# Cross attention: the subtraction of the row minima on GpSimd, one exponential a unit, and all transpose copies on ScalarE

## The chip, the cores and the metric

The kernel runs on one core of a Trainium2 chip. The metric is the device time of one launch in microseconds; the time before is the median of three runs. Five engines work side by side, each through its own instructions in order: TensorE (PE in the profile, its weight loads as PEld), VectorE (DVE), ScalarE (ACT), GpSimd (POOL) and SyncE (SP, which here issues DMAs). TensorE writes to PSUM[...]; GpSimd does not read PSUM in this kernel.

## The reference

One decoder layer, all in float32, for 4 batches of 1024 tokens with 256 features: a self attention made of three parts, a cross attention to 154 context rows with a distance bias, and a mixture of 8 experts with 2 for each token and a shared one. Each is followed by a residual sum and a layer norm. The change touches the cross attention alone:

```python
q = (query @ Wq.T + bq) * d ** (-0.5)      # 16 heads of 16 features
k = key_ @ Wk.T + bk                       # 154 rows
v = value @ Wv.T + bv
scores = jnp.einsum('bhqd,bhkd->bhqk', q, k)
distance_bias = -jnp.log(distances + 1e-09) * jnp.abs(distance_scaling)
scores = scores + distance_bias[:, None, :, :]
attn = jax.nn.softmax(scores, axis=-1)
out = jnp.einsum('bhqk,bhkd->bhqd', attn, v)
```

## The kernel before

The batches follow one another. Each has its self attention (long loops of score matmuls, exponentials and products), then a closing norm, then the cross attention, then a second norm. The experts come at the end, from about 2770 us on.

The cross attention of a batch is a loop over 32 units and 4 more steps (L951). A unit n is one pair of heads and one pair of token tiles: group n // 8 of four heads, token pair (n % 8) // 2, head pair n % 2. A step n emits, in this order: the scores of unit n; now and then the query projection of the next group (`project_q`, after units 3, 11 and 19); `flip` of unit n-2; on odd steps `product` of units n-5 and n-4; one piece of the next batch's beginning (`ahead`: score maxima and value projections, not in the last batch); and what the step counter `clock` has due, the `divide` of an earlier product.

`scores` (L654) makes four matmuls of 128 rows by 154 columns into one of two big PSUM buffers, which `maxima` and the projections of `ahead` use too. `biased` (L267, called at L673) is one VectorE instruction for each of the four 154-column parts (DVE L269): it reads the scores from PSUM, adds the bias, writes the negated sum to the tile `xs` and its minimum to a column of `xmx`. Four exponentials on ScalarE (L682) then work in place on `xs`, each with its own minimum as bias and scale -1, so that each gives exp(score - maximum).

`flip` (L691) transposes the unit on TensorE (L697), four 128x77 blocks into each of two small PSUM buffers (c = 0 and 1), and copies each to the tile `xpt`, 77 rows by 512 columns: on ScalarE (L705), except for c = 1 of odd units, which VectorE copies (L703). There are three small buffers, shared with `divide`, `values` and others. `product` (L708) multiplies two units by the values (L716), ScalarE copies the result to `avx` (L724), and `divide` (L348) transposes it back (L351) and divides it by the sums on VectorE (L354, L355).

The order on each engine is not only the source's. The framework orders instructions by the place in the source and by its own estimate of when each is ready and its buffer free, and writes the waits itself. Tiles of one kind share a ring of buffers: `xs`, `xpt` and the tiles of self attention share ten, `xmx` has three.

GpSimd adds the output bias to the residual just ahead of the loop (L747, eight instructions) and clears the values' tile of the next batch after it (L924). ScalarE takes the logarithm of the next batch's distances (L942) near the loop's end; the exponential and the logarithm need different function tables, each loaded by an ACT_TABLE_LOAD.

## Time and profile before

| | us |
|---|---|
| median of 3 runs (3431.95 to 3436.01) | 3435.27 |
| the profiled execution | 3433.82 |
| its span | 3432.0 |
| TensorE busy | 3300.5 |
| VectorE busy | 1725.3 |
| ScalarE busy | 1601.0 |
| GpSimd busy | 373.3 |
| first to last cross-attention score matmul, batch 0 | 632.3 to 737.4 |
| the same, batches 1, 2 and 3 | 1320.2 to 1423.6, 2006.3 to 2109.9, 2669.4 to 2754.1 |

A group's line in the profile reads: source line, engine, operation, tiles written and read, shapes, count, then after the bar the busy time and the mean in ns of one, then the idle time of that engine just ahead of it and what ended most of it. A line of the timeline reads: start, duration, engine, source line, operation, tiles, shapes, count, and in brackets the idle time and its releaser. The matmuls' ends are modelled, so that a busy TensorE need not be one at its peak. The granted clock of TensorE is 1.00 at full speed and 0.50 at half.

### The profile page before, as it was taken

How to read it: one execution, taken by the hardware profiler on the slowest of the kernel's cores; microseconds unless marked ns; L12 is line 12 of the kernel's file. 1: busy time of each engine (PE TensorE's matmuls, PEld its weight loads, DVE VectorE, ACT ScalarE, POOL GpSimd, SP SyncE). 2: the span in 40 equal slices, each digit the busy share in tenths (PEclk: the TensorE clock that was granted, in tenths of full speed). 3: DMA queues.
4: the chain of work that ended last, by engine and by line, in shares of the span. 5: the costliest groups of instructions: out<-in, count | busy, mean ns of one | idle time of the engine just before them, and what ended most of it. 6: DMA issues, size and time to landing. Idle time of an engine off the chain costs nothing.

```text
span 3432.0 us, 60936 instructions
## 1 busy us (share of the span) xinstructions
PE 3300.5 (96%) x25260; PEld 2085.6 (61%) x25260; DVE 1725.3 (50%) x3571; ACT 1601.0 (47%) x3130; POOL 373.3 (11%) x601
## 2 busy tenths in 40 slices
PE   7999999999999999999999999999999999999997
PEld 4555667565556675665566756555667665555554
DVE  3565555565655555656555556565556551122224
ACT  1555534375555453755554537555534731222223
POOL 4000000000000000000000000000000018222123
PEclk7999999999999999999999999999999999999999
DMA  9000000000000000000000000000000052111114
GB/s 204 1 2 1 1 1 1 3 21 14 1 1 1 1 1 3 21 13 2 1 1 1 1 3 9 1 2 1 1 1 1 1 203 82 47 42 44 44 44 157
DMA packets 75866, 84.13 MB, mean 25 GB/s; under 512 B 15136, under 2 KB 65928, under 8 KB 75592
## 3 DMA queue, kind: packets, MB, share of 16 engines
q1 hardware_dynamic: 68040, 61.53, 6.4%
q0 software_dynamic: 7552, 18.70, 1.6%
q8 instruction: 202, 3.31, 0.4%
q14 instruction: 72, 0.59, 0.1%
HBM read 46.52 MB, written 33.69 MB: 23 GB/s over the span
## 4 chain that ended last, share of the span: by engine, by line
PE 85%; DVE 9%; ACT 2%; issue 2%; POOL 1%; DMA 1%; SPq 0%; ACTq 0%; DVEq 0%; POOLq 0%
PE big L288 10%; PE big L422 8%; PE big L530 8%; PE one L566 7%; PE acc L584 7%; PE big L1226 7%; PE one L480 7%; DVE mxp L429 6%; PE one L460 4%; PE acc L1248 4%; PE one L697 3%; PE big L1178 3%; PE big L662 3%; PE one L302 2%; PE acc L716 2%
## 5 line engine op out<-in xcount | busy, mean ns | idle before, releaser
L429 DVE TENSOR_REDUCE mxp<-big 128x2 f32<-128x1024 f32 x512 | 610.3, 1218 | 305.5 <-PE acc L460 252.1
L422 PE MATMUL big<-k,q 31*128 31x512 f32 x2048 | 595.8, 644 | 30.2 <-DVE mxp L429 26.6
L471 ACT ACTIVATE ex<-one 128x512 f32<-128x512 f32 x696 | 391.3, 601 | 247.4 <-PE acc L460 182.9
L460 PE MATMUL one<-q,k 32*128 32x256 f32 x2784 | 501.9, 397 | 0.0
L269 DVE CUSTOM_DVE_ANT_0 prob<-big,zero_t 128x1024 f32<-128x1024 f32 x256 | 303.6, 1222 | 271.9 <-PE big L530 271.7
L460 PEld LDWEIGHTS one<-q,k 32*128 32x128 f32 x2784 | 326.8, 186 | 31.0 <-ACT ex L471 2.5
L549 ACT ACTIVATE prob<-prob,nmx 128x1024 f32<-128x1024 f32 x256 | 293.0, 1153 | 20.2 <-DVE nmx L269 19.7
L530 PE MATMUL big<-mk,mq 64*128 64x512 f32 x1024 | 284.4, 633 | 2.5 <-ACT ex L468 2.5
L422 PEld LDWEIGHTS big<-k,q 31*128 31x128 f32 x2048 | 180.1, 189 | 171.5 <-DVE mxp L429 93.6
L571 ACT COPY pt<-one 128x512 f32<-128x512 f32 x256 | 137.8, 588 | 311.7 <-PE one L566 311.7
L566 PEld LDWEIGHTS one<-ident,prob 128*128 128x128 f32 x2048 | 221.8, 142 | 98.1 <-issue 92.4
L1226 PE MATMUL big<-wall,xt 128*128 x576 | 272.5, 596 | 1.8 <-POOL by L1202 1.8
L460 PE MATMUL acc<-q,k 32*128 32x256 f32 x928 | 263.9, 404 | 0.0
L566 PE MATMUL one<-ident,prob 128*128 128x128 f32 x2048 | 257.6, 279 | 0.0
L480 PE MATMUL one<-ex,v 128*32 128x256 f32 x4096 | 248.4, 382 | 0.0
L1236 DVE TENSOR_TENSOR hidr<-big,slr 128x512 f32<-128x512 f32 x72 | 49.8, 691 | 332.7 <-ACT slr L1234 332.7
L682 ACT ACTIVATE xs<-xs,xmx 128x154 f32<-128x154 f32 x512 | 174.4, 414 | 69.6 <-DVE xmx L269 69.6
L480 PEld LDWEIGHTS one<-ex,v 128*32 128x32 f32 x4096 | 119.8, 110 | 122.1 <-ACT ex L471 35.8
L573 DVE COPY pt<-one 128x512 f32<-128x512 f32 x256 | 164.3, 683 | 10.9 <-PE one L566 10.9
L269 DVE CUSTOM_DVE_ANT_0 xs<-big,bias 128x154 f32<-128x154 f32 x512 | 132.0, 314 | 66.0 <-ACT avx L724 33.5
L530 PEld LDWEIGHTS big<-mk,mq 64*128 64x128 f32 x1024 | 99.6, 191 | 101.7 <-issue 79.4
L460 PEld LDWEIGHTS acc<-q,k 32*128 32x128 f32 x928 | 155.4, 186 | 0.0
(266 smaller groups left out, 4715.2 us busy)
## 6 DMA issues: line engine op xcount, KB each, us to landing
xg<-scratch SPq DMA_DIRECT2D x72, 129.0 KB, 2.0
scratch<-empty SPq DMA_DIRECT2D x1, 9216.0 KB
r<-result SPq DMA_DIRECT2D x8, 1024.0 KB, 11.2
y<-in_x_dram SPq DMA_DIRECT2D x4, 1024.0 KB, 5.3
wall<-in_L_ffn_w_gate_dram SPq DMA_DIRECT2D x8, 512.0 KB, 10.3
wall<-in_L_ffn_w_up_dram SPq DMA_DIRECT2D x8, 512.0 KB, 10.8
wall<-in_L_ffn_w_down_dram SPq DMA_DIRECT2D x8, 512.0 KB, 11.6
bias<-in_fside_BxSxS_dram SPq DMA_DIRECT2D x4, 616.0 KB, 4.5
```

Source lines behind the costliest of these rows:

```text
L269: nc.vector.tensor_tensor_reduce(out=out, in0=ps, in1=bias, scale=-1.0, scalar=3.0e38, op0=ALU.add, op1=ALU.min, accum_out=low,)
L288: nc.tensor.matmul(ps[:, tb, :], w[:, c, lo : lo + P], xT[:, c, tb * 512 : (tb + 1) * 512], start=(c == 0), stop=(c == NC2 - 1),)
L422: nc.tensor.matmul(ps[:, jj, :], st["q"][r : r + MR, tok : tok + P], st["k"][r : r + MR, kb * 512 : (kb + 1) * 512], start=True, stop=True,)
L429: nc.vector.reduce_max(mxp[:, t, kb, 2 * pair : 2 * pair + 2], ps, axis=AX.X)
L460: nc.tensor.matmul(scs[jj][:, i * QW : (i + 1) * QW], st["k"][r : r + MR + 1, kc * P : (kc + 1) * P], st["q"][r : r + MR + 1, part * QW : ...
L471: nc.scalar.activation(ex[:, jj, :], scs[jj], AF.Exp, scale=1.0 / HD**0.5)
L480: nc.tensor.matmul(av[32 * j : 32 * j + 32, 0:QW], self.v[:, kc, h * VW : h * VW + 32], exs[kc // 2, j // 2][:, j % 2, i : i + QW], start= ...
L530: nc.tensor.matmul(pss[i][:, kb, :], q[r : r + MD, t * P : (t + 1) * P], k[r : r + MD, kb * 512 : (kb + 1) * 512], start=True, stop=True,)
L549: nc.scalar.activation(p, p, AF.Exp, bias=nmx[:, i : i + 1], scale=-1.0, accum_out=sm[:, t % 4, i : i + 1],)
L566: nc.tensor.transpose(ps[:, kc * P : (kc + 1) * P], probs[u][i][:, at : at + P], ident)
L584: nc.tensor.matmul(av[64 * i : 64 * i + 64, (t % 4) * P : (t % 4 + 1) * P], v[:, kc, h * MD : (h + 1) * MD], flipped[u][i][:, kc, :], star ...
L1226: nc.tensor.matmul(ps[:, g, :], xt[:, c * P : (c + 1) * P], wall[:, bass.ds(off + (g * NC2 + c) * D, D)], start=(c == 0), stop=(c == NC2 - 1),
```

## The change

In `scores`, the minima tile `xmx` takes the order of `xs` (head, then token tile). One GpSimd instruction replaces `xs`, all four parts or 616 columns at once, by minimum minus negated score; the minima are read as a broadcast. One ScalarE exponential over the 616 columns, with neither bias nor scale, replaces the four. In `flip`, ScalarE makes both copies of every unit.

```diff
                 ex = ex_tile([P, 2, 2, S2], "xs")
-                mx = work.tile([P, 4], F32, tag="xmx", name="xmx", bufs=3)
+                mx = work.tile([P, 2, 2], F32, tag="xmx", name="xmx", bufs=3)
                 for tt in range(2):
                     for jj in range(2):
                         biased(
                             ex[:, jj, tt, :],
                             ps[:, jj, tt * S2 : (tt + 1) * S2],
                             self.bias[:, 2 * tp + tt, :],
-                            mx[:, 2 * tt + jj : 2 * tt + jj + 1],
+                            mx[:, jj, tt : tt + 1],
                         )
-                for tt in range(2):
-                    for jj in range(2):
-                        i = 2 * tt + jj
-                        nc.scalar.activation(
-                            ex[:, jj, tt, :],
-                            ex[:, jj, tt, :],
-                            AF.Exp,
-                            bias=mx[:, i : i + 1],
-                            scale=-1.0,
-                        )
+                nc.gpsimd.tensor_tensor(
+                    ex, mx.unsqueeze(3).to_broadcast([P, 2, 2, S2]), ex, ALU.subtract
+                )
+                nc.scalar.activation(ex, ex, AF.Exp)
                 self.ex[n] = ex
...
-                    if c == 1 and n % 2 == 1:
-                        nc.vector.tensor_copy(pt[0:HK, c, :], ps[0:HK])
-                    else:
-                        nc.scalar.copy(pt[0:HK, c, :], ps[0:HK])
+                    nc.scalar.copy(pt[0:HK, c, :], ps[0:HK])
```

## The prediction

> **What bounds the kernel now.** I read the page's busy shares first.

> ```profile
> PE 3300.5 (96%) x25260; PEld 2085.6 (61%) x25260; DVE 1725.3 (50%) x3571; ACT 1601.0 (47%) x3130; POOL 373.3 (11%) x601
> ```

> TensorE (PE) is busy nearly all the time. But shares average over stages, and the edit sits in one: the cross-attention loop, which runs four times from the first score matmul (L662) to the last product (L716), at 632.3, 1320.2, 2006.3 and 2669.4 us. The stage table cuts the first of these loops (columns: length, then busy time of PE, PEld, DVE, ACT, POOL, then the granted clock).

> ```profile
> 632.60:636.00 3.40, 2.04 (x22) 1.02 (x18) 3.17 (x17) 2.43 (x5) 0.00 (x0) 1.00 0.00 0
> 636.00:649.70 13.70, 13.70 (x39) 7.13 (x40) 5.21 (x24) 5.15 (x15) 0.00 (x0) 0.50 0.01 1
> 649.70:700.00 50.30, 49.95 (x387) 32.36 (x385) 30.84 (x135) 27.87 (x75) 0.00 (x0) 1.00 0.00 1
> 700.00:742.00 42.00, 41.96 (x409) 29.61 (x408) 26.41 (x149) 35.17 (x98) 0.00 (x0) 1.00 0.05 12
> ```

> See three phases. A head of 3.4 us in which PE idles 1.36 us. A body with no PE idle to speak of: until about 700 the next batch's matmuls are interleaved ("filled" units), after that the units stand alone ("bare") and ACT is busy 84%. And PE at half clock for 13.7 us right after the head. Is PE really the limit in the bare part, where ACT is at 84%? The chain of waits answers (start, us, what):

> ```profile
> 711.87 1.03 PE one L697 x8
> 713.12 0.72 PE big L662 x8
> 713.85 1.09 PE one L697 x8
> 714.94 1.00 PE acc L716 x16
> 715.94 0.72 PE big L662 x8
> ```

> Two units take 716.66 - 711.87 = 4.79 us, all PE: transposes, scores, transposes, product, scores, with 0.22 us for the divide's transposes at 712.90. ACT and DVE never enter. So ACT's 84% is cover, not limit.

> [...] The trace has 0.50 after a head with only 40% idle[...]; the lengths (13.7, 10.2, 10.2 and 6.8 us in the four loops) are multiples of 3.4. [...]

> **The change part by part.** There are 4 x 32 = 128 units.

> ```profile
> L682 ACT ACTIVATE xs<-xs,xmx 128x154 f32<-128x154 f32 x512 | 174.4, 414 | 69.6 <-DVE xmx L269 69.6
> L705 ACT COPY xpt<-one 77x512 f32<-77x512 f32 x192 | 104.3, 571 | 52.4 <-PE one L697 52.4
> L942 ACT ACTIVATE bias<-bias,tiny_t 128x1232 f32<-128x1232 f32 x4 | 5.3, 1322 | 7.6 <-DMA bias<-in_fside_BxSxS_dram 7.6
> ```

> ACT: four exponentials of 154 columns run in 1.36 us a unit. One of 616: between 154 columns (0.414) and 1232 (1.322) the slope is 0.842 ns a column, so 0.414 + 462 x 0.842 = 0.80 us. Saved 128 x 0.56 = 72 us. Moved to ACT are 64 copies at 0.571: 37 us added. ACT falls by 35 us net. DVE loses the 64 copies at 0.684: 44 us.

> ```profile
> L493 POOL TENSOR_TENSOR avq<-avq 128x256 f32<-128x256 f32 x64 | 46.3, 723 | 956.5 <-ACT avq L488 956.5
> L1293 POOL TENSOR_TENSOR r<-r,r 128x2048 f32<-128x2048 f32 x4 | 21.7, 5424 | 14.1 <-DMA r<-result 14.1
> ```

> POOL gains 128 subtractions of 616 columns: slope (5424 - 723)/1792 = 2.62 ns, so 0.723 + 360 x 0.00262 = 1.67 us each, 213 us in all. Broadcasting should cost nothing: POOL's copy of a broadcast 128x512 (L599) takes 613 ns, a plain one (L1124) 615. Bounds: 0.74, if the minima cost no second read (L599's 613 ns plus 104 columns at 1.2), to 2.64, if POOL stood still during DVE's 0.97 us a unit. At 2.39 us a bare unit POOL is 70% full; at 2.64 it would be the bound itself, +0.25 us on some 80 bare units, +20 us, which the range below takes in.

> All of the 35 and 44 us lies beside PE in the body, so it buys nothing. What is left is latency. Count from the end of unit n's scores. Before: 0.16 to DVE, exponentials trailing DVE by one; the last ends at about +1.9. After: DVE's four minima end at 0.16 + 1.04 = 1.20; handoff 0.16; POOL 1.67; handoff 0.12; exponential 0.80; handoff to PE 0.16: transposes may start at +4.11. They are wanted after unit n+2's scores, at +4.79. So 0.68 us is left in the bare part, and about 3 in the filled part (two units take 7.1 there, from 667.07 to 674.18). An excess x would delay only every third unit's cycle, since two more scores stand before these transposes on PE.

> Who queues behind the new wait? On ACT, the copies of unit n-2, which free PE's transpose buffers (three). If an exponential that waits for POOL stood ahead of them, they would end about +4.5 instead of 1.6 and PE would stop. In the trace the framework's order follows readiness and not the source: at 664.57 one exponential, then a copy, then three exponentials; and at 669.68 a divide's transposes lie between halves of one unit's scores. The copies are ready at +0.6, the exponential not before +2.9, so I expect the copies ahead. On POOL nothing else falls in the loop but the end of eight bias additions (626.27 to 631.79), done before the first minimum at 634.2; the next batch's memset (L924) comes after it. The c=1 copies of odd units end on ACT at about +3.6 or 4.4, before PE wants the buffer. Body: 0.

> Head: the first four exponentials ended at 636.2. Now DVE 634.2, POOL to 636.0, exponential to 636.9, or 638.1 if the 1.28 us table load is also behind the wait. PE has the next batch's maxima and values to run instead, except in the last loop. Bounds -1.4 (the idle time goes) to +3; I take +0.3 a loop. Tail: unit 31's scores ended at 737.78, so its transposes start at 737.78 + 4.11 = 741.9 and not 741.17, +0.7; its two copies are now both on ACT, +0.5 at most, and ahead of the table load and logarithm at 742.53 that hold up the last average copy. I take +0.8, between 0 and 1.5. Sum: 4 x (0.3 + 0.8) = +4.4. The profiled execution took 3433.82 (span 3432.0, 1.8 around it), 1.45 below the median of 3435.27. So 3433.8 + 4.4 = 3438.2, say **3438**, with its own range of 3429 to 3442.

> **The rivals.**
> Rival 1, **faster by the clock**: the four half-clock stretches sum to 13.7 + 10.2 + 10.2 + 6.8 = 40.9 us, costing up to 20.5. They follow heads where PE waited on single exponentials (0.29 us twice) and minima (0.78). If the new order puts other matmuls there, the head's 1.4 goes and the stretches shrink. All of it: -26; half: -13, 3421. For it: next batch's matmuls are ready in three loops. Against: the 0.78 us wait is for DVE's minima in a score buffer and stays.
> Rival 2, **slower, late ends and a cold clock**: head +3, tail +1.5, and one more half-clock window at each (1.7 us each): 4 x (4.5 + 3.4) = 32 at most, half of it +16: 3450. It decides once PE idles over about 1.4 us in 3.4, as the head does now.
> Rival 3, **slower, the new wait on ACT**: exponential n ahead of the copies of n-2. Then copies end at +4.5, the next unit's transposes and product follow (1.7 + 1.0), scores 0.72: two units take about 7.3 instead of 4.79, +2.5. Bare pairs: some 8 in each of three loops and 14 in the last, 38 in all: +95, 3529; fewer pairs give less. A subtraction beyond 1.67 + 0.68 = 2.35 us would begin a smaller stall, a third of the excess a unit.
> That the change does not do what it says has little room: the instructions are written out.

> **How the numbers follow.** Within 0.2% (6.9 us), about what a measurement of this kernel can tell from no change. My forecast 0.41, rival 1 0.27, rival 2 0.22, rival 3 0.10. The range runs from 3416 (two thirds of rival 1) to 3465 (rival 2 whole); it leaves out the end of rival 1 (0.06) and most of rival 3 (0.09). Faster 0.27, same 0.40, slower 0.33: one hundredth of the forecast's own range spills over.

> **What would show it.** Right: two bare units still 4.79 us on PE; POOL near 1.67 and ACT near 0.80 us each; copies of n-2 ahead of exponential n. Wrong: PE idle at L697 on ACT in the body (rival 3), a half-clock stretch gone or longer at the heads (rivals 1 and 2), or POOL above 2.35.

## The result and the profile after

| | before | after |
|---|---|---|
| median of 8 runs each, us | 3433.38 (3431.26 to 3436.79) | 3448.60 (3442.02 to 3452.80) |
| the profiled execution, us | 3433.82 | 3444.80 |
| its span, us | 3432.0 | 3443.0 |
| mean granted clock of TensorE in it | 0.976 | 0.973 |

After over before is 1.0042, 95% interval 1.0031 to 1.0053: slower, by about 15 us at the medians. The profiled execution after lies 3.8 us below its median, so the traces have 11.0 us to explain.

Two words for what follows: the head of a batch's loop is its first few microseconds, the tail what lies behind its last scores. The change shortens the file, so the same lines have smaller numbers after: L697 becomes L691, L716 L707, L724 L715 and L942 L933.

First the page of the kernel after, its line of busy shares.

```profile
PE 3311.8 (96%) x25260; PEld 2090.0 (61%) x25260; DVE 1684.3 (49%) x3507; ACT 1560.0 (45%) x2810; POOL 529.6 (15%) x729
```

See that three engines moved as meant: ACT lost 41 us and DVE 41, POOL gained 156. PE is busy 11.3 us longer with the same 25260 matmuls. The same matmuls took longer, and that is what a lower clock looks like, not a wait: in the kernel before, the eight 31x512 matmuls of L422 from 636.0 to 649.7 us, at a granted clock of 0.50, took 1137 ns on average, the sixteen from 649.7 to 700, at 1.00, 640 ns.

Next, the groups of instructions of the kernel after: the subtraction that is new.

```profile
L679 POOL TENSOR_TENSOR xs<-xmx,xs 128x616 f32<-128x616 f32 x128 | 155.3, 1214 | 243.3 <-DVE xmx L269 180.7
```

1.21 us each. Does PE wait for it, or for the exponential behind it? The chain of waits of the kernel after, in the bare part of batch 0 (start, us, what):

```profile
711.41 0.72 PE big L662 x8
712.14 1.03 PE one L691 x8
713.17 0.33 PE one L351 x2
713.50 0.72 PE big L662 x8
714.22 1.03 PE one L691 x8
715.25 1.00 PE acc L707 x16
716.25 0.72 PE big L662 x8
```

It is all PE, as before. Two units take 716.25 - 711.41 = 4.84 us. In PE's list of waits the transposes of the exponentials (L691) do not appear; of the loop's own lines the one that grew is the divide's transpose (L351), which waits for the copy of the average: from 4.3 us in 5 waits to 6.4 us in 6. The longest, 1.1 us before and 1.6 after, is at the tail. The timeline of the kernel after, at the end of batch 0's cross attention (start, us, engine, line, operation):

```profile
738.50 1.07 ACT L696 COPY xpt<-one 77x512 f32<-77x512 f32 x2 [0.36 <-PE one L691]
...
738.83 1.07 PE L707 MATMUL acc<-xpt,vx 77*32 77x256 f32 x16
739.59 1.28 ACT L933 ACT_TABLE_LOAD   x1
...
739.83 1.13 PE L422 MATMUL big<-k,q 31*128 31x512 f32 x4
740.88 1.32 ACT L933 ACTIVATE bias<-bias,tiny_t 128x1232 f32<-128x1232 f32 x1
742.11 0.35 ACT L715 COPY avx<-acc 128x256 f32<-128x256 f32 x1
...
742.52 0.65 PE L351 MATMUL one<-ident,avx 128*128 128x128 f32 x2 [1.55 <-ACT avx L715]
```

Read it from the bottom. PE idles 1.55 us for a copy (L715) of 0.35. The product that the copy reads ended at 739.9; ACT is then in the table load and logarithm of the next batch's bias, which came first. They in turn wait for the two copies of unit 31's transposes, now both on ACT. The same place before:

```profile
742.25 1.07 PE L716 MATMUL acc<-xpt,vx 77*32 77x256 f32 x16
...
742.53 1.28 ACT L942 ACT_TABLE_LOAD   x1
...
745.05 0.35 ACT L724 COPY avx<-acc 128x256 f32<-128x256 f32 x1
...
745.46 0.44 PE L351 MATMUL one<-ident,avx 128*128 128x128 f32 x2 [1.08 <-ACT avx L724]
```

There the table load began 0.28 us after the product (742.25 to 742.53), now it begins 0.76 us after it (738.83 to 739.59): 0.48 us later, and the idle time grew from 1.08 to 1.55.

Then the clock. The stage table of the kernel after around that gap (length, busy time of PE, PEld, DVE, ACT, POOL, then the granted clock, DMA share, GB/s):

```profile
739.20:742.60 3.40, 1.84 (x21) 0.52 (x11) 0.36 (x1) 3.23 (x4) 0.00 (x0) 1.00 0.00 0
742.60:763.10 20.50, 20.50 (x69) 12.71 (x70) 5.33 (x12) 6.21 (x10) 0.58 (x1) 0.50 0.00 0
```

Behind the window in which PE was busy 1.84 of 3.40 us, half clock follows, for 20.5 us. And the same place before:

```profile
741.20:744.60 3.40, 3.18 (x28) 1.55 (x28) 1.16 (x3) 3.04 (x4) 0.00 (x0) 1.00 0.47 142
744.60:748.00 3.40, 2.54 (x21) 1.04 (x22) 2.40 (x4) 1.17 (x3) 0.57 (x1) 1.00 0.00 0
```

No half clock followed here. I added up every half-clock stretch of both traces:

| half clock, us | before | after | change |
|---|---|---|---|
| heads of the four loops | 13.7, 10.2, 10.2, 6.8 | 10.2, 0, 13.7, 3.4 | -13.6 |
| after the first three tails | 0, 0, 3.4 | 20.5, 10.2, 13.7 | +41.0 |
| everywhere else | 120.0 | 116.5 | -3.5 |
| all | 164.3 | 188.2 | +23.9 |

I count half of a half-clock stretch as lost, an estimate from the granted 0.50 for a PE that is busy throughout: +12.0 us. (By L422's 640 and 1137 ns it would be 0.44 of a stretch, +10.5 us.) The loops bear it out. With half of 13.7, 10.2 and 10.2 us taken off, the first three loops before come to 98.6, 98.7 and 98.9 us from first to last score matmul; with half of 10.2, 0 and 13.7 taken off, those after come to 96.6, 96.8 and 96.4. With the clock taken out in this way the whole kernel before has 3349.9 us and after 3348.9. So the 11.0 us are 12.0 of clock less 1.0 of everything else.

### The profile page after: what moved, and what is told of

Read it like the earlier page. It is cut to its first block, busy times and chain, and to the rows that moved or that the text cites. A ratio compares the mean times of both kernels' runs of the same rounds, so it can differ in the third digit from the quotient of the medians.

```text
span 3443.0 us, 60727 instructions
## 1 busy us (share of the span) xinstructions
PE 3311.8 (96%) x25260; PEld 2090.0 (61%) x25260; DVE 1684.3 (49%) x3507; ACT 1560.0 (45%) x2810; POOL 529.6 (15%) x729
## 4 chain that ended last, share of the span: by engine, by line
PE 83%; DVE 9%; POOL 3%; issue 2%; DMA 2%; ACT 1%; SPq 0%; ACTq 0%; DVEq 0%; POOLq 0%
PE big L288 10%; PE big L422 8%; PE big L530 8%; PE one L566 7%; PE acc L584 7%; PE big L1217 7%; PE one L480 7%; DVE mxp L429 6%; PE one L460 4%; PE acc L1239 4%; PE one L691 4%; PE big L662 3%; PE one L302 2%; PE acc L707 2%; PE big L630 2%
## 5 line engine op out<-in xcount | busy, mean ns | idle before, releaser
L422 PE MATMUL big<-k,q 31*128 31x512 f32 x2048 | 594.5, 641 | 31.1 <-DVE mxp L429 27.4
L269 DVE CUSTOM_DVE_ANT_0 prob<-big,zero_t 128x1024 f32<-128x1024 f32 x256 | 303.6, 1222 | 272.4 <-PE big L530 272.2
L422 PEld LDWEIGHTS big<-k,q 31*128 31x128 f32 x2048 | 179.5, 188 | 172.2 <-DVE mxp L429 94.5
L493 POOL TENSOR_TENSOR avq<-avq 128x256 f32<-128x256 f32 x64 | 46.4, 725 | 960.2 <-ACT avq L488 960.2
L679 POOL TENSOR_TENSOR xs<-xmx,xs 128x616 f32<-128x616 f32 x128 | 155.3, 1214 | 243.3 <-DVE xmx L269 180.7
L269 DVE CUSTOM_DVE_ANT_0 xs<-big,bias 128x154 f32<-128x154 f32 x512 | 132.2, 314 | 86.4 <-PE big L662 86.2
L573 DVE COPY pt<-one 128x512 f32<-128x512 f32 x256 | 164.3, 683 | 9.7 <-PE one L566 9.6
```

Source lines behind the costliest of these rows:

```text
L269: nc.vector.tensor_tensor_reduce(out=out, in0=ps, in1=bias, scale=-1.0, scalar=3.0e38, op0=ALU.add, op1=ALU.min, accum_out=low,)
L422: nc.tensor.matmul(ps[:, jj, :], st["q"][r : r + MR, tok : tok + P], st["k"][r : r + MR, kb * 512 : (kb + 1) * 512], start=True, stop=True,)
```

## The experiments

The leading theory, called the clock theory in the expectations or A, says: PE's idle time at the tail, made by the table load and logarithm ahead of the last average's copy on ACT, turns the clock down. B says that GpSimd's subtraction makes units late. C says that the wait or the order of the instructions itself costs, without the clock. Each run was compared with the kernel before on the same chip; before's median there was between 3434.5 and 3436.5 us.

### The logarithm held back, in the kernel after

```diff
-            nc.scalar.activation(bf, bf, AF.Ln, bias=tiny_t)
+            tiny_y = work.tile([P, 1], F32, tag="tinyy", name="tinyy", bufs=1)
+            nc.vector.tensor_scalar(tiny_y, y[:, 0, 0:1], 0.0, 1e-9, ALU.mult, ALU.add)
+            nc.scalar.activation(bf, bf, AF.Ln, bias=tiny_y)
```

The constant is made from the next batch's first normalised row, times zero, so the logarithm can't start before that row is there: in this kernel's trace, ahead of the second loop, the constant is written at 1297.55 us and the logarithm starts at 1297.72. No table load follows the row (ACT idled for the 5.64 us ahead of the logarithm), and none stands in ACT's list at the first tail, from 737 to 746 us.

> The changed kernel, but the logarithm of the distances takes its small constant from this batch's normed tokens (times 0, plus 1e-9), so that it can't start before the first norm closes; the table load and logarithm leave the loop's tail. Theory A (TensorE idles 1.55 us at the tail behind the logarithm on ScalarE, and its clock is halved afterwards): the gap before the divide's transposes (L351) falls under 0.7 us, no half-clock stretch starts at a tail, granted clock 0.976 or more, 3425 to 3435 us, below the kernel before or equal. Theory B (the GpSimd step makes the loop's units late): nothing but the tail changes, 3443 to 3450.

Measured: 3426.72 us (3424.78 to 3434.10), ratio 0.9981, 0.9973 to 0.9989. The subtraction, the single exponential and all copies are as in the kernel after, and the 15 us are gone, with 7 more. Of the 18.8 us between the spans of the two traces, 17.7 are clock by the same count. The timeline of this kernel at the same tail:

```profile
738.90 1.07 PE L707 MATMUL acc<-xpt,vx 77*32 77x256 f32 x16
...
740.09 0.37 ACT L715 COPY avx<-acc 128x256 f32<-128x256 f32 x1 [0.50 <-PE acc L707]
...
740.95 0.44 PE L351 MATMUL one<-ident,avx 128*128 128x128 f32 x2
```

The copy follows its product at once, PE has no idle time in front of L351, and none of the three tails has half clock after it. B falls: the subtractions are all there. But this edit takes away the wait as well as the low clock, so A and C are not yet apart.

### Useless work in the gap, in the kernel after

The product of units 28 and 29 is computed three times over in the first three batches; the output stays the same.

```diff
-                for c in range(2):
-                    for j in range(4):
+                for _ in range(self.times if n == 29 else 1):
+                    for c in range(2):
+                        for j in range(4):
...
+            xa.times = 3 if b < B - 1 else 1
```

> The changed kernel with useless work: the product of units 28 and 29 is computed three times over in the first three batches, 2.0 us more matmuls in each tail, in the place where TensorE waits 1.55 us for ScalarE. The logarithm stays where it is. Theory A (the wait halves the clock): the gap is filled, the half-clock stretches at the tails go, and the kernel gets faster by doing more: 3428 to 3438 us, clock 0.976. Theory C (it is the wait itself and the order of the tail's work that cost, not the clock): no gain, 3448 to 3454.

Measured: 3432.95 us (3427.12 to 3435.68), ratio 0.9992, 0.9984 to 1.0000. The timeline and the stage table of this kernel at the tail:

```profile
739.13 2.80 PE L708 MATMUL acc<-xpt,vx 77*32 77x256 f32 x48
739.88 1.28 ACT L934 ACT_TABLE_LOAD   x1
741.17 1.32 ACT L934 ACTIVATE bias<-bias,tiny_t 128x1232 f32<-128x1232 f32 x1
...
742.40 0.35 ACT L716 COPY avx<-acc 128x256 f32<-128x256 f32 x1
...
742.90 0.44 PE L351 MATMUL one<-ident,avx 128*128 128x128 f32 x2
```

```profile
739.50:742.90 3.40, 3.40 (x50) 1.46 (x38) 0.37 (x1) 3.22 (x4) 0.00 (x0) 1.00 0.00 1
742.90:746.30 3.40, 3.40 (x30) 1.89 (x30) 2.50 (x6) 0.44 (x2) 0.57 (x1) 1.00 0.00 0
```

The logarithm still stands ahead of the copy on ACT, and the copy is as late as ever (3.3 us after its product began; 3.3 in the kernel after). Only PE's idle time is filled, with 32 matmuls that nobody needs, and the kernel is 15.7 us faster at the medians. None of the three tails has half clock after it. The tail up to the last product takes 10.5 us, about what it takes at full clock in the kernel after (10.3). So whatever the wait's own length costs is still paid in this kernel, and the loss is gone all the same: what made it was the clock. C falls as the cause of the 15 us. (PE's order at the tail moved a little with it: fewer of the next batch's L422 stand ahead of the divide.)

### Each half of the change alone

All copies on ScalarE, in the kernel before, with its four exponentials:

```diff
-                    if c == 1 and n % 2 == 1:
-                        nc.vector.tensor_copy(pt[0:HK, c, :], ps[0:HK])
-                    else:
-                        nc.scalar.copy(pt[0:HK, c, :], ps[0:HK])
+                    nc.scalar.copy(pt[0:HK, c, :], ps[0:HK])
```

> The other part alone: four exponentials as before, all copies on ScalarE. Theory A: ScalarE reaches the table load later, the gap is 1.5 us or more and half-clock stretches start at the tails: 3440 to 3452. Theory B: as the kernel before, 3431 to 3436.

Measured: 3453.44 us (3451.57 to 3455.93), ratio 1.0056, 1.0043 to 1.0070. The stage table of this kernel at the first tail:

```profile
743.90:747.30 3.40, 1.79 (x21) 0.91 (x20) 1.96 (x3) 1.78 (x4) 0.15 (x1) 1.00 0.00 0
747.30:761.00 13.70, 13.70 (x43) 8.80 (x42) 3.06 (x8) 5.01 (x8) 0.42 (x1) 0.50 0.00 0
```

1.61 us of idle time and 13.7 us of half clock at each of three tails. The time is 1.4 us above the upper end of A's range, and B falls. The copies alone cost at least what the whole change does. Not all of it is clock: with the clock taken out this trace has 3354.6 us, 4.7 more than the kernel before, whose tails are about 1.6 us shorter (9.1 against 10.7).

The other half is the kernel after with the copies as they were (the same lines, turned round): subtraction and single exponential alone.

> The GpSimd subtraction and the single exponential alone: the copies are those of the kernel before (odd units, second half, on VectorE). Theory A: one copy less stands ahead of the table load, the gap is about 1.1 us instead of 1.55 and the clock is mostly kept: 3430 to 3438. Theory B: as the changed kernel, 3445 to 3450.

Measured: 3440.88 us (3429.30 to 3446.95), ratio 1.0019, 1.0011 to 1.0027, above what A expected and below what B did. The idle time at the tails is back at 1.08, half clock there is 6.8, 3.4 and 6.8 us. With the clock taken out its trace has 3349.3 us, so the subtraction makes nothing late. But the profiled run is the shortest of the 16, 11.6 us below their median; the granted clock of the others goes down to 0.972, and no trace shows where they lost it.

### One copy a batch

If the tail is what counts, 4 of the 64 moved copies should matter, those of unit 31. In the kernel before, this one alone to ScalarE:

```diff
-                    if c == 1 and n % 2 == 1:
+                    if c == 1 and n % 2 == 1 and n < 31:
```

> The kernel before, with one copy a batch moved: the second copy of unit 31's transposes goes from VectorE to ScalarE (4 of the 64 copies that the change moves). Clock theory: the copy at the tail is the one that counts; the idle time ahead of the last average's transposes goes from 1.08 to about 1.6 us at three tails, half clock of about 13 us follows at each, and the time is 3445 to 3454, as with all 64 copies moved. The theory that the copies cost by their number or by their order in the units: at most a tenth of the loss, 3434 to 3437, with no half clock at the tails.

Measured: 3438.76 us (3429.26 to 3460.53), ratio 1.0014, 1.0002 to 1.0027. It lies above the range of the second theory and below that of the first, whose size was missed: idle time at the tails 1.57 us, as expected by A, but half clock of only 3.4, 3.4 and 10.2 us. The stage table of this kernel at the first tail shows why so little:

```profile
741.70:745.10 3.40, 2.73 (x26) 1.15 (x24) 0.06 (x1) 3.08 (x4) 0.00 (x0) 1.00 0.30 92
745.10:748.50 3.40, 2.50 (x21) 0.99 (x22) 2.40 (x4) 1.22 (x3) 0.57 (x1) 1.00 0.00 0
748.50:751.90 3.40, 3.40 (x17) 3.40 (x18) 0.50 (x2) 1.43 (x3) 0.00 (x0) 0.50 0.00 0
```

Within each trace, all half-clock stretches begin on one grid of 3.41 us (all 20 in that of the kernel before, all 21 in that of the kernel after). Here the idle time, 744.4 to 746.0, lies across a line of that grid, and each window keeps a busy share of 0.74 to 0.80. In the kernel with all copies moved it lay within one window at each tail (share 0.53), and in the kernel after at the first and third tail (20.5 and 13.7 us) but not the second (10.2). Here it lies within one at the third tail only, the one with 10.2 us. In the kernel before, the shorter gap of 1.08 us lies across a line at all three tails (0, 0 and 3.4 us followed); in the run with the subtraction alone, the same gap lies within one window at each (6.8, 3.4 and 6.8). So in these traces what followed a gap went with its length and with its place. The wide spread of these runs, whose clock went from 0.969 to 0.978, may come from that too; no run shows it. (The grid's place in the program isn't the same in every execution: two traces of one kernel, in a later section, have it 1.7 us apart.) I did not set the phase, so this is read from traces and not shown by an edit.

In the kernel after, the same copy alone back to VectorE:

```diff
-                    nc.scalar.copy(pt[0:HK, c, :], ps[0:HK])
+                    if c == 1 and n == 31:
+                        nc.vector.tensor_copy(pt[0:HK, c, :], ps[0:HK])
+                    else:
+                        nc.scalar.copy(pt[0:HK, c, :], ps[0:HK])
```

> The kernel after, with one copy a batch moved back: the second copy of unit 31 on VectorE. Clock theory: the idle time at three tails falls to about 1.1 us, the half clock after the tails shrinks as it did with all 64 copies moved back, and the time is 3430 to 3442. The theory that the change costs by its copies or its subtraction in the body of the loop: 3445 to 3451, as after.

Measured: 3432.23 us (3418.88 to 3439.56), ratio 0.9985, 0.9976 to 0.9994. One copy a batch takes back the loss: 16 us at the medians. The idle time is 1.08 us. The traces tell less: of the 12.2 us by which its span is shorter than that of the kernel after, 7.3 are clock and 4.9 are not (1.5 of these in the tails, the rest I have not placed). Its profiled execution still has 6.8, 3.4 and 13.7 us of half clock at the tails, with a window of share 0.68 ahead of the first:

```profile
741.60:745.00 3.40, 2.32 (x24) 0.78 (x16) 1.34 (x3) 2.52 (x3) 0.00 (x0) 1.00 0.00 0
745.00:751.80 6.80, 6.80 (x32) 4.40 (x24) 1.81 (x5) 2.06 (x4) 0.57 (x1) 0.50 0.00 0
```

### The logarithm held back, in the kernel before

With the three lines of the first experiment:

> The kernel before with the same edit to the logarithm. Theory A: its tail gap of 1.08 us goes too; it had a half-clock stretch at one tail of three in the profile, so 2 to 6 us less than before: 3427 to 3432. Theory B says nothing of it: 3429 to 3434, one microsecond a tail.

Measured: 3438.64 us (3428.40 to 3443.90), ratio 1.0010, 1.0003 to 1.0017. A miss. The idle time of 1.08 us is gone and no tail has half clock, yet the median is no better. There was little to gain: the kernel before has 3.4 us of half clock at its tails. Its profiled execution took 3429.86 us, and another profiled one of the same kernel 3427.13:

> The kernel before with the logarithm moved, once more, for a second trace: its runs reach from 3428 to 3444 us with nothing idle at the tails. Theory A: the runs differ in the half-clock stretches that start at the heads and in the self attention, by their place in a fixed grid of 3.4 us; with the clock taken out (span less half of the half-clock time) this trace gives 3349 to 3351 us, as the first one did (3349.9).

This missed too. The 3349.9 counted the last half-clock stretch beyond the end of the span; so counted, the second trace has 3347.6. Counted to the end of the span, as in the table above, the first has 3351.0 and the second 3348.7. Of the 2.8 us between the two spans only 0.6 is clock; the rest is small differences that the clock doesn't explain. Both traces are among its shortest runs, and both have no half clock at the head of batch 2's loop (the third of the four). Over its 21 runs span times clock is 3348.6 us at the median, against 3349.3 for the kernel before, so most of what its longer runs lose is clock (0.973 to 0.978). Where the clock fell in them no trace shows: open.

With all copies on ScalarE as well:

> The kernel before, with all copies on ScalarE and the logarithm held back until the first normalised row. Clock theory: no idle time of over 0.3 us at three tails, no half clock there, and the time is that of the kernel before with the logarithm held back, 3430 to 3441. If the copies cost by themselves: 3450 to 3456, as with all copies on ScalarE and the logarithm where it was.

Measured: 3433.33 us (3428.12 to 3436.65), ratio 0.9994, 0.9986 to 1.0002. Moving the 64 copies cost 19 us where the logarithm stood ahead of the last average, and nothing where it didn't (3438.64 without them moved). None of its three tails has half clock. The stage table of this kernel at the first tail, to be held against that of the copies alone:

```profile
738.50:741.90 3.40, 3.40 (x29) 1.79 (x28) 0.50 (x2) 1.73 (x4) 0.00 (x0) 1.00 0.30 91
741.90:745.30 3.40, 3.40 (x28) 1.71 (x28) 1.92 (x5) 0.37 (x1) 0.57 (x1) 1.00 0.00 0
```

### A longer tail, in the kernel before

A useless copy of the bias on itself, to make the tail's wait longer:

```diff
+            nc.scalar.copy(bf, bf)
             nc.scalar.activation(bf, bf, AF.Ln, bias=tiny_t)
```

> The kernel before with one useless copy of the 1232 distances on ScalarE (1.3 us) ahead of the logarithm. Nothing of the change is in it. Theory A: TensorE idles longer at three tails, half-clock stretches of 6 to 14 us start there, 3442 to 3455 us. Theory B or C: three times at most 1.3 us, 3434 to 3438.

Measured: 3433.73 us (3429.25 to 3438.30), ratio 0.9996, 0.9988 to 1.0004. A miss, and no test: the average's copy found its place between the two, and the idle time became 1.24, 0.51 and 0.30 us instead of longer at all three. Behind the first, the longest, 3.4 us of half clock follow (748.4 to 751.8), behind the other two none.

### Useless work at the heads as well

If half clock at the heads costs in the same way, matmuls that fill their idle time should gain. In the first experiment's kernel, after the scores of unit 1:

```diff
+                    if n == 1:
+                        warm = acc()
+                        for i in range(8):
+                            nc.tensor.matmul(
+                                warm[:, 0:QW], ident, x1T[:, 0, 0:QW], start=True, stop=True
+                            )
```

> The changed kernel with the logarithm moved as in the run before, and eight useless matmuls of 256 columns (2.1 us) after the scores of unit 1 in every batch, where TensorE waits for the first minima and exponentials. Theory A: the heads' half-clock stretches (10.2 to 13.7 us in each of four) shrink or go: up to 20 us below 3426.7, 3406 to 3424. Theory C: 4 to 8 us of added work, 3428 to 3436.

Measured: 3424.94 us (3422.75 to 3426.91), ratio 0.9968, 0.9957 to 0.9980, the shortest median of all. The stage table of this kernel at its first head:

```profile
633.80:637.20 3.40, 2.92 (x18) 2.38 (x18) 2.51 (x13) 0.72 (x1) 2.02 (x2) 1.00 0.00 0
637.20:640.60 3.40, 3.40 (x22) 1.94 (x21) 1.84 (x5) 0.72 (x1) 0.41 (x1) 1.00 0.00 0
```

Half clock is gone from three heads, where the first experiment's trace has 10.2, 13.7 and 13.7 us. But each of these loops now takes 99.95 us where its full-clock length was 97.5: 2.5 us of added work a loop against the 5 to 7 that the clock returns. In the traces the two cancel: 10.8 us less lost to the clock than in the first experiment's trace, 11.0 us more of everything else, and spans of 3424.4 against 3424.2 us. The 1.8 us between the medians are not clear of noise, for the intervals of the two ratios overlap. So the clock can be bought back at the heads too, but this much added work costs as much as it brings, and the expectation's upper end (3424) was missed for that.

## Why the prediction was right or wrong

3438 was forecast, 3448.6 measured: inside the range of 3416 to 3465, outside the likeliest case's own 3429 to 3442, and slower by more than 0.2%, which had a chance of 0.33. That it lies in the range is owed to rival 2 and not to the sum. Of the sum's terms the body was right, the tail right in kind and too small, the head wrong in sign, and the clock at the tails was not in it.

**"Body: 0"** was right. Bare pairs stayed all PE (4.84 us in the piece shown, 4.79 before), and the 41 us off ACT and 41 off DVE bought nothing there. The latency count was generous: POOL's subtraction took 1.21 us and not 1.67, the exponential 0.72 and not 0.80. The 1.67 was an estimate, a slope of 2.62 ns an element between two rows of other shapes. Here, with the minima read as a broadcast, the time came out midway between the lower bound of 0.74 us and the 1.67 taken; that the broadcast is the reason no run tested. The other bound, 2.64 us with POOL standing still while DVE works, was an assumption and did not show: all 128 subtractions took 1213 to 1217 ns, and DVE's scores-plus-bias 314 ns on average as before.

**"Head +0.3 a loop"** had the wrong sign. At full clock the four loops took 96.6, 96.8, 96.4 and 81.3 us after, 98.6, 98.7, 98.9 and 81.6 before: 6.8 us less in all. The first three loops hold as many matmuls as before (813 each), and PE's idle time in them fell from between 1.7 and 1.9 us to 1.12. The term that the prediction feared, the 1.28 us table load behind the new wait, went the other way: before, it stood behind the first minima (633.56 in batch 0); after, it ran at 627.59, six microseconds ahead of the first subtraction. The rest of the 6.8 us I didn't separate.

**"Tail +0.8 a loop"** named the right mechanism: two copies on ACT, ahead of the table load and logarithm, hold up the last average's copy, and the +0.5 I gave the second copy was measured as 0.48. The tails grew by 1.1 to 1.3 us at full clock instead of 0.8; in the first three, 0.47 of that is idle time, and two more of the next batch's matmuls (L422, seven instead of five) stand in each. Loops and tails together made -2.0 where my sum had +4.4.

**What failed is that the forecast left the clock at the tail at nothing.** The tail's term was summed as waiting time alone, and what the wait set off, 41.0 us of half clock after three tails, weighs 20.5 us, nearly five times the whole sum. Rival 2 had it in kind: idle time over "about 1.4 us in 3.4" turns the clock down, an estimate from the 1.36 us of the one head ahead of its 0.50; the tail reached 1.56 in 3.40. It put the new half clock at heads and tails alike, one window each. The new half clock came at the tails alone, as three to six windows, while the heads gave back 13.6 us of it (6.8 us of rival 1's gain). Its half size, 3450, is close to the measured time through these two errors against each other.

I had both numbers for it in hand: 1.36 us of idle time at the head with half clock after it, 1.08 at the tail with none after two of three, and +0.5 on the latter. That makes 1.58, above the head's 1.36.

**Rival 3** did not come about: no exponential held up an older unit's copies to PE's cost; PE has no wait at L691 in its list.

**What stays open:** the exact condition of the clock. Windows of 1.79, 1.84, 2.32 and 2.68 us of 3.40 were followed by half clock, 2.50 once was, 2.54 was not, and 2.74 was in the kernel after at its second tail; the ends of matmuls are modelled, so these shares are not exact. They are not the whole condition either. Before the last batch's loop in the kernel before, a window of 1.87 us (2667.0 to 2670.4) was not followed by half clock. And the half clock from 793.8 in the kernel after follows windows of 3.12 and 3.40 us. That the idle gaps at the tails brought half clock (20.5, 10.2 and 13.7 us behind them in the kernel after), and filled ones did not (none behind any of three), is shown by the edits; how long and where a gap must be is not. Open too is where the longer runs of two kernels lose their clock: the one before with the logarithm held back, and the one with the subtraction alone.

## What to carry to other kernels

Where TensorE is the limit, price an added wait on it twice: its own length, and the half clock that may follow it (here 0.47 us more in each of three tails, and 41.0 us more at 0.50 after them). Compare it with gaps of that length in the same trace that were or were not followed by half clock; this gives a suspicion, not a threshold. An edit that fills the gap with useless matmuls and leaves the wait where it is tells the two costs apart. A step on another engine that frees nothing on the critical path (here one copy of 0.6 us a batch) can cost through the last instructions of a stage, so read the tail's queue instruction by instruction. What needs no result early, such as the next batch's logarithm with its table load, belongs behind the stage's last copies; this one edit turned a loss of 0.4% into a gain of 0.2% in the kernel after, and gained nothing in the kernel before, whose tails had hardly lost any clock.
